# Cross attention with its queries in front of the sums and a group's output products together; self-attention with wide scores and a joined side step

## The chip, the cores and the metric

The kernel runs on one NeuronCore of a Trainium2 chip. The metric is the device time of one execution in microseconds (us), the median of three runs. A core has five engines that each take their instructions in order: TensorE (PE: matrix products; PEld is its loading of the stationary operand), VectorE (DVE), ScalarE (ACT), GpSimd (POOL) and SyncE (SP, which only issues DMAs here). TensorE writes its results to PSUM, eight banks of 2 KiB on each of 128 partitions; VectorE and ScalarE read them from there. GpSimd works on the on-chip memory (SBUF) alone.

## The reference

The program is a decoder of four layers. Each layer has an attention, a cross attention and a feed-forward part, and after each the residual is added and the rows are normalized. The input `x` has 16 batches of 256 tokens with 128 features; the context `ctx_1024` has 64 tokens a batch. Everything is computed in fp32 as far as this change is concerned.

Three cross attentions, in layers 0, 2 and 3, have 16 heads of 8 features and a softmax over the 64 context tokens. In layer 3 the cross attention is followed by a self-attention over the 256 tokens of a batch, also with 16 heads of 8 features:

```python
q = _split_heads(x @ qw + qb)
k = _split_heads(ctx @ kw + kb)
v = _split_heads(ctx @ vw + vb)
scores = jnp.einsum('bqhd,bkhd->bhqk', q, k) / np.sqrt(D // H).astype(np.float32)
...
probs = jax.nn.softmax(scores, axis=-1)
out = jnp.einsum('bhqk,bkhd->bqhd', probs, v)
```

`ca = _mha(input_tensor, ctx_tensor, ...)` gives the cross attention, `sa = _mha(x, x, ...)` the self-attention; each is followed by an output product, residual and normalization.

## The kernel before

The program is written stage by stage on one core. `x` stays on the chip twice: `xt` holds tokens on partitions, `xT` holds features on partitions. Tokens are worked on in 8 groups of 512, a group being two batches. Two stages are concerned.

**`cross_attention` (line 523)** serves the three cross attentions: `layer_x0` (with `side`, which puts the end of layer 0's recurrence, `scan` and `turn`, between the steps), `layer_x2`, and `layer_last` (with a mask and an extra scaling of the scores, lines 582 to 585). Its loop runs over batches `b`, with six steps more at the end. A step does:

- `scores(b + 1)`: for each of four 32-row strips `i` and two halves `u`, a product of 32 rows (heads 4i to 4i+3) with the masked keys `kb` as stationary operand and 256 query columns. `kb`, made by GpSimd in `keys`, holds the keys four times, each time with all but one head of a strip set to zero. The result fills two PSUM tiles `sc` of two banks; ScalarE takes the exponential into `e`.
- `settle`: the last step of a pending normalization (line 404 on ScalarE, 407 on VectorE).
- `sums(b)`: numerators (`vx` as stationary operand) and denominators (a constant) for all heads into one bank `nd`; `normalized` (line 1966) takes the reciprocal `rcT` and multiplies into `oTn`, both on VectorE.
- `keys(b + 2)`; at even `b` `queries(b // 2 + 1)`, a product of 512 columns and its eviction to `qT` on VectorE; at `b % 4 == 1` `values`, four products and their evictions into `vx`.
- `out_product` (line 635) for batch `b - 1`: two products with the output weights into half of bank `y`; after the second batch of a group, `finish` adds the residual (`r`) and starts the normalization, whose reciprocal root (line 383) is on GpSimd.
- `transposed`: four transposes of a finished group and a copy to `xT` on ScalarE.

PSUM is divided by tags. Each call takes four banks for `sc` and one for `y`; with `side` one for `nd` and two for `m`, without `side` two for `nd` and one for `m`. `queries`, `values` and `transposed` share `m`.

**`self_attention` (line 1856)** takes four steps `j` for each batch `n`, each with four heads. A step issues the scores of the next step, then `aside(n, j)`, then its sums. `scores(n, j)` makes eight products, for two halves `t` of the keys and four strips `i`: masked keys `kb[n][r, j, 128 t: ...]` as stationary operand, 256 query columns moving. `sums` makes eight products into `nd`; after the fourth step `nd` is copied (`nds`), the denominators' reciprocal `rcs` is made on VectorE and the numerators are put together in `vas` on GpSimd. `aside` holds everything else, each piece with one bank `m` for all:

- `divided(n - 1)` at `j == 1`: a product with a constant (`swap`) brings the reciprocals to their rows; VectorE multiplies into `oTs`.
- `batch(n + 1)` at `j == 2`: the value product, its evictions into `vs` (four on VectorE), and the masked keys `kb` (one GpSimd instruction, line 1894).
- `project` at even `n`: keys of the next group at `j == 0`, queries at `j == 3`.
- at odd `n`: `out` at `j == 0`, `transposed` at `j == 3`.

Order on TensorE is written out by hand: inside `in_order` every matrix instruction is chained to the one before it (`put`, line 304). The order on the other engines is made by a scheduler when the program is built; the hand-written marks `behind` only add to it. A pool of `bufs` tiles is used in turn, and a new tile waits for all readers of the one before it in the same buffer. `work` tiles have two buffers unless another number is given.

Of the kernel before, what the change touches and what calls it, by code (L numbers as in the profile page):

```python
# [16 lines left out]
ALU = mybir.AluOpType  # L17
# [5 lines left out]
NG = NT // 512  # L23
# [499 lines left out]
def cross_attention(s, wq, wk, wv, wo, bq, bk, bv, finish, mask=None, side=None):  # L523
# [14 lines left out]
    q, kb, es, oT, y = {}, {}, {}, {}, {}  # L538
# [58 lines left out]

    if side is None:
        side = lambda b, late: None
        few, more = 2, 1  # L600
    else:
        few, more = 1, 2
    with s.banks(sc=(2, 2), nd=(few, 1), y=(1, 1), m=(more, 1)), s.in_order(), s.deferring():
# [11 lines left out]
        for b in range(B + 6):  # L615
# [3 lines left out]
            side(b, False)  # L619
            if b < B:  # L620
                sums(b)
            side(b, True)
            if b + 2 < B:
                keys(b + 2)
                if b % 2 == 0:
                    queries(b // 2 + 1)
                if b % 4 == 1 and b + 3 < B:
                    values(b // 4 + 1)
            if 1 <= b <= B:
                out_product(s, y, oT, b - 1, wo, finish)  # L630
            if b % 2 == 1 and b >= 5 and b // 2 - 2 < NG:
                s.transposed(b // 2 - 2)


def out_product(s, y, oT, b, wo, finish):

    if b % 2 == 0:
        y[b // 2] = s.bank("y", [128, 4, D])
    for t in range(2):
        s.mm(y[b // 2][:, 2 * (b % 2) + t, :], oT[b][:, 128 * t:128 * t + 128], wo)  # L640
    if b % 2 == 1:
        finish(b // 2, y[b // 2])
# [1213 lines left out]
def self_attention(s, wq, wk, wv, wo, bq, bk, bv, finish):  # L1856
# [7 lines left out]

    nc = s.nc
# [10 lines left out]
    q, k, kb, es, oT, nd, va, rc = {}, {}, {}, {}, {}, {}, {}, {}  # L1876
# [7 lines left out]
    def batch(n):  # L1884
        ps = s.bank("m", [128, 2, 256])
        for t in range(2):
            s.mm(ps[:, t, 0:128], s.xT[:, S * n + 128 * t:S * n + 128 * t + 128], wv)
        pv = ps[:, :, 0:128].rearrange("p t (i j d) -> p t i j d", i=4, j=4)
# [3 lines left out]
        kb[n] = s.work("kb4", [128, 4, S])  # L1892
        o = S * (n % 2)
        nc.gpsimd.tensor_tensor(kb[n], k[n // 2][:, o:o + S].unsqueeze(1).broadcast_to([128, 4, S]), hm4, ALU.mult)

    def scores(n, j):
        o = S * (n % 2)
        sc = [s.bank("sc", [128, 2, 2, S]) for _ in range(2)]
        for t in range(2):
            for i in range(4):  # L1900
                r = slice(32 * i, 32 * i + 32)
                s.mm(sc[i // 2][:, i % 2, t, :], kb[n][r, j, 128 * t:128 * t + 128], q[n // 2][r, o:o + S])
# [4 lines left out]
    def sums(n, j):  # L1907
        if j == 0:
            nd[n] = s.bank("nd", [128, 2, S])
        for t in range(2):  # L1910
# [27 lines left out]
    def aside(n, j):  # L1938

        g = n // 2  # L1940
        if j == 1 and 1 <= n <= B:
            divided(n - 1)
        if j == 2 and n + 1 < B:
            batch(n + 1)
# [63 lines left out]
```

## Time and profile before

| what | us |
|---|---|
| median of the runs (2226.88, 2229.49, 2230.01) | 2229.49 |
| the profiled execution's own time | 2229.6 |
| its span from the first instruction to the last | 2227.8 |
| TensorE busy in the span | 1795.3 |
| reciprocals `rcT` in the cross attentions, 48 of 1751 ns | 84.1 |
| exponentials `e` of the self-attention, 128 of 1021 ns | 124.0 |
| VectorE `rcs` reciprocals of the self-attention, 16 of 1753 ns | 28.0 |

The page of the profile gives busy time per engine and groups of equal instructions by line, engine, tile and shape. A group's row reads: count, busy time, mean length of one in ns, then the engine's idle time just before them and what ended it. `out<-in` names the tile written and the tiles read. An fp32 product appears as two records, each with its own load of the stationary operand. `32*128 32x256` means a stationary operand of 32 rows by 128 columns and a moving one of 32 rows by 256 columns. Two kinds of query are used besides: the waits (who waited for whom, total, times, longest) and the timeline (start, length, engine, line, tiles, count, and in brackets the engine's idle time before it with its releaser). TensorE's clock is granted in two rates; the share granted is a column of the busy time by stretch. Ends of matrix products are modelled, so lengths overlap, and steps are best read from start to start.

### The profile page before, as it was taken

The page shows a single profiled execution, that of the slowest core. Times are in us where ns is not written, and L with a number is a line of the kernel's source. Part 1 is how long each engine was busy: PE and PEld are TensorE (multiplying, and loading weights), DVE is VectorE, ACT ScalarE, POOL GpSimd, SP SyncE. Part 2 cuts the span into 40 slices and gives each one's busy share as a digit, 9 for nine tenths or more (in the row PEclk, how much of TensorE's full clock was granted, in tenths as well). Part 3 has the DMA queues.
Part 4 walks back from the last instruction along what each step waited for, and adds up shares of the span by engine and source line. Part 5 has one row for each costly group of instructions (what it writes and reads, how often), then busy time and mean ns, then how long its engine had stood idle before and what let it go on. Part 6 is the DMA issues. An engine that isn't in the chain of part 4 may idle for free.

```text
span 2227.8 us, 39433 instructions
## 1 busy us (share of the span) xinstructions
PE 1795.3 (81%) x16572; PEld 1132.3 (51%) x16572; DVE 1133.0 (51%) x2808; ACT 857.9 (39%) x1267; POOL 811.0 (36%) x956
## 2 busy tenths in 40 slices
PE   6784388886999836949784789987789988999998
PEld 3451256664777624625452556654445544555554
DVE  5677624544366663145476677746725552322231
ACT  6565633432333201322354222225646653223221
POOL 2432322222244325755434334444536652111110
PEclk8896569997999956969896899988979998999999
DMA  3000000001011221430000000010000000000000
GB/s 114 4 3 21 1 2 3 3 3 45 1 30 29 71 51 45 76 88 0 6 14 20 1 1 1 2 41 23 2 1 2 2 1 1 5 5 5 5 10 10
DMA packets 45649, 41.59 MB, mean 19 GB/s; under 512 B 6880, under 2 KB 42144, under 8 KB 44832
## 3 DMA queue, kind: packets, MB, share of 16 engines
q1 hardware_dynamic: 35456, 31.22, 4.5%
q0 software_dynamic: 5632, 4.33, 1.5%
q10 hardware_dynamic: 4384, 3.52, 0.5%
q8 instruction: 130, 2.13, 0.4%
q14 instruction: 47, 0.39, 0.1%
HBM read 28.44 MB, written 10.62 MB: 18 GB/s over the span
## 4 chain that ended last, share of the span: by engine, by line
PE 56%; DVE 18%; POOL 11%; issue 7%; ACT 5%; DMA 2%; POOLq 0%; DVEq 0%; SPq 0%; ACTq 0%
PE p L336 14%; PE m L336 12%; PE sc L336 11%; PE y L336 6%; PE nd L336 3%; POOL rs L383 2%; PE nd L340 2%; PE den L340 2%; DVE rcT L1969 2%; PE m L343 2%; POOL acc L1318 2%; PE num L336 2%; DVE st L393 1%; ACT xt L404 1%; DVE r L458 1%
## 5 line engine op out<-in xcount | busy, mean ns | idle before, releaser
L336 PE MATMUL p<-h,w_f 128*128 128x512 f32 x512 | 222.3, 592 | 0.4 <-DVE h L1820 0.4
L336 PE MATMUL sc<-qT,kb 32*128 32x256 f32 (+1 forms) x2816 | 184.3, 381 | 42.6 <-DVE qT L650 17.2
L381 POOL TENSOR_SCALAR ve<-mv 128x4 f32<-128x4 f32 x128 | 30.6, 239 | 427.1 <-DVE mv L394 423.7
L336 PEld LDWEIGHTS sc<-qT,kb 32*128 32x128 f32 x2816 | 129.6, 204 | 94.3 <-issue 61.2
L343 PE MATMUL m<-ident,xt 128*128 128x128 f32 x448 | 87.8, 318 | 104.0 <-ACT xt L404 47.4
L336 PEld LDWEIGHTS p<-h,w_f 128*128 128x128 f32 x512 | 96.7, 190 | 119.8 <-issue 117.9
L1905 ACT ACTIVATE e<-sc 128x1024 f32<-128x1024 f32 x128 | 124.0, 1021 | 74.2 <-PE sc L336 73.4
L383 POOL TENSOR_TENSOR rs<-ve,nhalf 128x4 f32<-128x4 f32 x128 | 134.3, 1049 | 6.3
L343 PEld LDWEIGHTS m<-ident,xt 128*128 128x128 f32 x448 | 59.1, 156 | 132.9 <-ACT xt L404 54.8
L393 DVE BATCH_NORM_STATS2 st<-r 128x6 f32<-128x128 f32 x480 | 119.6, 272 | 3.3
L435 POOL TENSOR_TENSOR xb<-xt,r_x 128x512 f32<-128x512 f32 x48 | 60.8, 1271 | 152.2 <-DVE r L1763 76.9
L1969 DVE RECIPROCAL rcT<-nd 128x256 f32<-128x256 f32 x48 | 84.1, 1751 | 62.3 <-PE nd L336 62.3
L355 ACT COPY xT<-m 128x512 f32<-128x512 f32 x104 | 60.0, 581 | 139.2 <-PE m L343 138.5
L404 ACT ACTIVATE xt<-r,nm,rs 128x128 f32<-128x128 f32 x176 | 72.5, 484 | 95.0 <-POOL nm L399 95.0
L1825 ACT ACTIVATE h<-p,w_f 128x512 f32<-128x512 f32 x64 | 44.0, 687 | 153.6 <-PE p L336 153.5
L336 PE MATMUL m<-xT,w_a 128*128 128x512 f32 x144 | 82.0, 685 | 25.7 <-DVE vxs L910 18.9
L407 DVE TENSOR_SCALAR xt<-r,mv,rs 128x128 f32<-128x128 f32 x208 | 66.8, 382 | 59.6 <-POOL rs L383 59.6
L1831 DVE TENSOR_TENSOR ys<-y,r_f 128x512 f32<-128x512 f32 x8 | 5.5, 691 | 175.4 <-PE y L336 175.4
L578 ACT ACTIVATE e<-sc 128x1024 f32<-128x1024 f32 x64 | 61.9, 1019 | 62.6 <-PE sc L336 62.6
L1626 DVE TENSOR_TENSOR a<-sc,cst 128x1024 f32<-128x1024 f32 x64 | 75.0, 1208 | 14.4 <-PE sc L336 14.3
L394 DVE BATCH_NORM_AGGREGATE mv<-st 128x2 f32<-128x6 f32 x512 | 80.7, 167 | 0.1
L1094 ACT ACTIVATE e<-sc 128x1024 f32<-128x1024 f32 x32 | 32.8, 1024 | 110.0 <-PE sc L336 110.0
(423 smaller groups left out, 4075.2 us busy)
## 6 DMA issues: line engine op xcount, KB each, us to landing
acc<-xt SPq DMA_DIRECT2D x16, 256.0 KB, 2.8
mw<-in_moe SPq DMA_DIRECT2D x8, 512.0 KB, 4.1
yx<-acc SPq DMA_DIRECT2D x12, 256.0 KB, 3.6
w_f<-in_w_f SPq DMA_DIRECT2D x1, 2824.0 KB, 10.5
w_x<-in_w_x SPq DMA_DIRECT2D x1, 2336.5 KB, 9.8
xt<-in_x SPq DMA_DIRECT2D x8, 256.0 KB, 7.5
rows<-xn SPq DMA_DIRECT2D x8, 256.0 KB, 2.5
out_x<-xt SPq DMA_DIRECT2D x8, 256.0 KB, 2.3
```

What stands on the lines that cost most here:

```text
L336: self.put(self.nc.tensor.matmul(out=out, lhsT=lhsT, rhs=rhs, start=start, stop=stop))
L340: self.put(self.nc.tensor.matmul(out=out, lhsT=lhsT, rhs=rhs, start=start, stop=stop, skip_group_check=True))
L343: self.put(self.nc.tensor.transpose(out, in_, self.ident if ident is None else ident))
L383: nc.gpsimd.tensor_tensor(rs, ve, self.nhalf[:, :n], ALU.pow)
L393: nc.vector.bn_stats(st[:, j, :], r[:, j, :])
L394: nc.vector.bn_aggr(mv[:, j, :], st[:, j, :])
L404: ins, front = nc.scalar.activation(out[:, j, :], r[:, j, :], AF.Identity, bias=nm[:, j:j + 1], scale=rs[:, j:j + 1]), self.latest
L407: ins, front = nc.vector.tensor_scalar(out[:, j, :], r[:, j, :], mv[:, j, 0:1], rs[:, j:j + 1], ALU.subtract, ALU.mult), self.mark
L578: s.latest = nc.scalar.activation(eu, sc[h], AF.Exp, scale=8 ** -0.5)
L1626: s.mark = nc.vector.tensor_tensor(a[:, h, :, :], sc[h].rearrange("p i j k -> p (i j) k"), tri, ALU.mult)
L1905: nc.scalar.activation(e[:, 2 * h:2 * h + 2, :, :], sc[h], AF.Exp, scale=8 ** -0.5)
L1969: s.nc.vector.reciprocal(rc, nd[:, 1, :])
```

## The change

In `cross_attention`, `queries(b // 2 + 1)` is issued between the scores of `b + 1` and the sums of `b`, at even `b`. The output products of a group's two batches are no longer made one batch a step but all four at the even step that follows the group's second batch, in a new `out`, ahead of `values` and `transposed`. The bank `y` is gone: `out` takes its bank from `m`, which has three banks with `side` and two without. `oTn` has three buffers.

In `self_attention`, queries are masked instead of keys (`qb`), and scores are made with 128 keys as stationary operand and the masked queries of two heads, 512 columns, as moving one: four products a step instead of eight. A step now covers half of the keys for two heads, where it covered all keys for one head of each strip; `sums` follows that. The value product of the next batch and the `swap` product of the last one are put in the two halves of one bank at `j == 1`, with `divided` and `batch` behind them. Queries are projected at `j == 0` and keys at `j == 2`.

```diff
@@ -535,7 +535,7 @@
         nc.gpsimd.memset(t, 0.0)
     on = s.c["on2"].rearrange("p (u k) -> p u k", u=2)
     hm4 = s.c["hm4"].unsqueeze(2).broadcast_to([128, 4, SC])
-    q, kb, es, oT, y = {}, {}, {}, {}, {}
+    q, kb, es, oT = {}, {}, {}, {}
 
     def values(g):
         ps = s.bank("m")
@@ -595,12 +595,16 @@
                          es[b][:, i, u, :], u == 0, u == 1)
         oT[b] = normalized(s, nd)
 
+    def out(g):
+        y = s.bank("m", [128, 4, D])
+        for j in range(4):
+            s.mm(y[:, j, :], oT[2 * g + j // 2][:, 128 * (j % 2):128 * (j % 2) + 128], wo)
+        finish(g, y)
+
+    few = 1
     if side is None:
-        side = lambda b, late: None
-        few, more = 2, 1
-    else:
-        few, more = 1, 2
-    with s.banks(sc=(2, 2), nd=(few, 1), y=(1, 1), m=(more, 1)), s.in_order(), s.deferring():
+        side, few = lambda b, late: None, 2
+    with s.banks(sc=(2, 2), nd=(few, 1), m=(4 - few, 1)), s.in_order(), s.deferring():
         side(-1, False)
         for g in range(2):
             ps = s.bank("nd")
@@ -617,29 +621,19 @@
                 scores(b + 1)
             s.settle()
             side(b, False)
+            if b % 2 == 0 and b + 2 < B:
+                queries(b // 2 + 1)
             if b < B:
                 sums(b)
             side(b, True)
             if b + 2 < B:
                 keys(b + 2)
-                if b % 2 == 0:
-                    queries(b // 2 + 1)
-                if b % 4 == 1 and b + 3 < B:
-                    values(b // 4 + 1)
-            if 1 <= b <= B:
-                out_product(s, y, oT, b - 1, wo, finish)
+            if b % 2 == 0 and 2 <= b <= B:
+                out(b // 2 - 1)
+            if b % 4 == 1 and b + 3 < B:
+                values(b // 4 + 1)
             if b % 2 == 1 and b >= 5 and b // 2 - 2 < NG:
                 s.transposed(b // 2 - 2)
-
-
-def out_product(s, y, oT, b, wo, finish):
-
-    if b % 2 == 0:
-        y[b // 2] = s.bank("y", [128, 4, D])
-    for t in range(2):
-        s.mm(y[b // 2][:, 2 * (b % 2) + t, :], oT[b][:, 128 * t:128 * t + 128], wo)
-    if b % 2 == 1:
-        finish(b // 2, y[b // 2])
 
 
 def evac_dve(s, out, ps, bias=None):
@@ -1873,7 +1869,7 @@
     hm4 = s.c["hm4"].unsqueeze(2).broadcast_to([128, 4, S])
     lo, hi = s.c["half"][:, 0:1], s.c["half"][:, 1:2]
     row = bv.rearrange("p (i j d) -> p i j d", i=4, j=4)
-    q, k, kb, es, oT, nd, va, rc = {}, {}, {}, {}, {}, {}, {}, {}
+    q, k, qb, es, oT, nd, va, rc = {}, {}, {}, {}, {}, {}, {}, {}
 
     def project(d, n, g, wt, bias):
         ps = s.bank("m")
@@ -1881,25 +1877,28 @@
         d[g] = s.work(n, [128, 512])
         evac_dve(s, d[g], ps, bias)
 
-    def batch(n):
-        ps = s.bank("m", [128, 2, 256])
+    def product(n, ps):
+        ps = ps.rearrange("p (t c) -> p t c", t=2)
         for t in range(2):
-            s.mm(ps[:, t, 0:128], s.xT[:, S * n + 128 * t:S * n + 128 * t + 128], wv)
-        pv = ps[:, :, 0:128].rearrange("p t (i j d) -> p t i j d", i=4, j=4)
+            s.mm(ps[:, t, :], s.xT[:, S * n + 128 * t:S * n + 128 * t + 128], wv)
+
+    def batch(n, ps):
+        ps = ps.rearrange("p (t c) -> p t c", t=2)
+        pv = ps.rearrange("p t (i j d) -> p t i j d", i=4, j=4)
         for j in range(4):
             nc.vector.tensor_tensor(vxs[n % 3][:, :, :, 40 * j:40 * j + 8], pv[:, :, :, j, :],
                                     row[:, :, j, :].unsqueeze(1).broadcast_to([128, 2, 4, 8]), ALU.add)
-        kb[n] = s.work("kb4", [128, 4, S])
+        qb[n] = s.work("kb4", [128, 4, S])
         o = S * (n % 2)
-        nc.gpsimd.tensor_tensor(kb[n], k[n // 2][:, o:o + S].unsqueeze(1).broadcast_to([128, 4, S]), hm4, ALU.mult)
+        nc.gpsimd.tensor_tensor(qb[n], q[n // 2][:, o:o + S].unsqueeze(1).broadcast_to([128, 4, S]), hm4, ALU.mult)
 
     def scores(n, j):
-        o = S * (n % 2)
+        o = S * (n % 2) + 128 * (j % 2)
         sc = [s.bank("sc", [128, 2, 2, S]) for _ in range(2)]
-        for t in range(2):
-            for i in range(4):
-                r = slice(32 * i, 32 * i + 32)
-                s.mm(sc[i // 2][:, i % 2, t, :], kb[n][r, j, 128 * t:128 * t + 128], q[n // 2][r, o:o + S])
+        for i in range(4):
+            r = slice(32 * i, 32 * i + 32)
+            s.mm(sc[i // 2][:, i % 2, :, :].rearrange("p h k -> p (h k)"), k[n // 2][r, o:o + 128],
+                 qb[n][r, j - j % 2:j - j % 2 + 2, :].rearrange("p h k -> p (h k)"))
         e = es[n, j] = s.work("e", [128, 4, 2, S])
         for h in range(2):
             nc.scalar.activation(e[:, 2 * h:2 * h + 2, :, :], sc[h], AF.Exp, scale=8 ** -0.5)
@@ -1907,10 +1906,12 @@
     def sums(n, j):
         if j == 0:
             nd[n] = s.bank("nd", [128, 2, S])
-        for t in range(2):
+        t = j % 2
+        for u in range(2):
             for i in range(4):
-                s.part(nd[n][32 * i:32 * i + 32, j // 2, :], vxs[n % 3][:, t, i, 32 * j:32 * j + 32],
-                       es[n, j][:, i, t, :], j == t == 0, j % 2 == 1 and t == 1)
+                h = j - t + u
+                s.part(nd[n][32 * i:32 * i + 32, j // 2, :], vxs[n % 3][:, t, i, 32 * h:32 * h + 32],
+                       es[n, j][:, i, u, :], j == u == 0, t == u == 1)
         if j == 3:
             sb = s.work("nds", [128, 2, S])
             nc.vector.tensor_copy(sb, nd[n])
@@ -1923,11 +1924,9 @@
                 nc.gpsimd.tensor_scalar(sb[:, u, :], sb[:, u, :], m, None, ALU.mult)
             nc.gpsimd.tensor_tensor(va[n], sb[:, 0, :], sb[:, 1, :], ALU.add)
 
-    def divided(n):
-        ps = s.bank("m", [128, 2, S])
-        s.mm(ps[:, 0, :], s.c["swap"], rc[n])
+    def divided(n, ps):
         oT[n] = s.work("oTs", [128, S], bufs=4)
-        nc.vector.tensor_tensor(oT[n], va[n], ps[:, 0, :], ALU.mult)
+        nc.vector.tensor_tensor(oT[n], va[n], ps, ALU.mult)
 
     def out(g):
         y = s.bank("m", [128, 4, D])
@@ -1938,12 +1937,17 @@
     def aside(n, j):
 
         g = n // 2
-        if j == 1 and 1 <= n <= B:
-            divided(n - 1)
-        if j == 2 and n + 1 < B:
-            batch(n + 1)
-        if n % 2 == 0 and j in (0, 3) and g + 1 < NG:
-            project(*((q, "qT", g + 1, wq, bq) if j else (k, "kTs", g + 1, wk, bk)))
+        if j == 1 and n <= B:
+            ps = s.bank("m", [128, 2, S])
+            if n + 1 < B:
+                product(n + 1, ps[:, 1, :])
+            if n >= 1:
+                s.mm(ps[:, 0, :], s.c["swap"], rc[n - 1])
+                divided(n - 1, ps[:, 0, :])
+            if n + 1 < B:
+                batch(n + 1, ps[:, 1, :])
+        if n % 2 == 0 and j in (0, 2) and g + 1 < NG:
+            project(*((q, "qT", g + 1, wq, bq) if j == 0 else (k, "kTs", g + 1, wk, bk)))
         if n % 2 == 1 and j == 0 and 1 <= g <= NG:
             out(g - 1)
         if n % 2 == 1 and j == 3 and 2 <= g <= NG + 1:
@@ -1952,7 +1956,9 @@
     with s.banks(sc=(3, 2), nd=(1, 1), m=(1, 1)), s.in_order():
         project(q, "qT", 0, wq, bq)
         project(k, "kTs", 0, wk, bk)
-        batch(0)
+        ps = s.bank("m", [128, 2, S])[:, 1, :]
+        product(0, ps)
+        batch(0, ps)
         scores(0, 0)
         for n in range(B + 4):
             for j in range(4):
@@ -1967,7 +1973,7 @@
 
     rc = s.work("rcT", [128, S], bufs=1)
     s.nc.vector.reciprocal(rc, nd[:, 1, :])
-    oT = s.work("oTn", [128, S])
+    oT = s.work("oTn", [128, S], bufs=3)
     s.nc.vector.tensor_tensor(oT, nd[:, 0, :], rc, ALU.mult)
     return oT
 
```

## The prediction

> **What bounds the kernel now.** I read the page's head first, then each engine's busy time in the four stretches that the diff touches, then TensorE's waits in each, then the order of its work inside one period.
>
> ```profile
> span 2227.8 us, 39433 instructions
> ...
> PE 1795.3 (81%) x16572; PEld 1132.3 (51%) x16572; DVE 1133.0 (51%) x2808; ACT 857.9 (39%) x1267; POOL 811.0 (36%) x956
> ```
> ```profile
> 67.00:176.00 109.00, 83.67 (x946) 52.29 (x946) 74.55 (x200) 59.73 (x100) 39.33 (x72) 0.91 0.03 8
> 1085.00:1182.00 97.00, 78.06 (x900) 46.11 (x898) 62.10 (x153) 46.25 (x69) 29.65 (x52) 0.93 0.06 20
> 1512.00:1624.00 112.00, 83.08 (x904) 48.06 (x904) 76.11 (x156) 69.58 (x89) 52.43 (x74) 0.88 0.00 1
> 1624.00:1826.00 202.00, 190.77 (x2255) 104.50 (x2255) 95.81 (x246) 127.13 (x135) 106.45 (x95) 0.96 0.01 2
> ```
> Columns of the second: stretch, its length, busy TensorE, weight loads, VectorE, ScalarE, GpSimd, granted clock, DMA. The rows are the cross attentions of layers 0, 2 and 3 (x0, x2, x3 below), then the self-attention. No DMA matters in them. Self-attention is TensorE-bound, 191 of 202 us. The cross attentions leave TensorE 19 to 29 us idle each, with VectorE 62 to 76 us busy. Who ends those waits in x2:
>
> ```profile
> PE sc L336 <- DVE qT L650: 8.9, 8, 1.3
> PE m L343 <- DVE vx L554: 3.9, 2, 1.9
> ```
> Scores wait each pair of batches for the queries' eviction (`qT`); a transpose waits twice for the one `m` bank that `values` still holds. x0 and x3 show 8.4 and 8.3 us of the first, x3 4.0 of the second. In self-attention the timeline of TensorE (start, length) shows one wait per two batches:
>
> ```profile
> 1698.88 1.15 PE L336 MATMUL sc<-qT,kb 32*128 32x256 f32 x16
> 1699.95 0.70 PE L336 MATMUL m<-rcs,cst 128*128 128x256 f32 x2
> 1700.58 1.07 PE L340 MATMUL nd<-e,vs 128*32 128x256 f32 x16
> 1701.58 1.15 PE L336 MATMUL sc<-qT,kb 32*128 32x256 f32 x16
> 1704.04 0.71 PE L336 MATMUL m<-w_x,xT 128*128 128x128 f32 x4 [1.31 <-DVE oTs L1930]
> 1704.68 1.07 PE L340 MATMUL nd<-e,vs 128*32 128x256 f32 x16
> ```
> From start to start: scores 1.08, sums 1.00, swap 0.63, value product 0.64. The product waits 1.31 us because the swap result in the same bank is read by `oTs`, which stands on VectorE behind the normalization (`r`, L407), which waits for GpSimd.
>
> **Self-attention, part by part.** *Wide scores.* Sixteen records of 256 columns become eight of 512, half the weight loads; streamed columns are the same. Four row groups start within 21 ns of each other, the next four 216 ns later; records of 512 columns in plain products follow each other every 429 ns (32 records `p<-h` take 13.90 us, the last 0.59 alone). So a phase changes from 4 x 216 to 2 x 429: 6 ns, times 64 = -0.4. [...] The trace shows each load begun while the row group before it streams, so I take 0.4. [...] The 256-column rows overlap fully; no row here has 32 rows by 512. [...]
> *Joined aside.* Value product and swap follow each other without the load-and-drain edge between a tiled and a full phase: a product before another full phase takes 0.54, before sums 0.64; 15 x 0.10 = -1.5. The product now stands before the swap, so it no longer waits for `oTs`: six waits (1.42 and five of 1.31) go, -8.0. Where does that stall go? `oTs` ends 4.03 us after the swap's start (1703.98 against 1699.95). The next user of `m` in an odd batch is now the transpose, about 1.17 + 2 x 2.08 = 5.3 us after the joined aside begins; `vs` adds 0.61, and the bank is free at about 5.1 at the latest. In an even batch it is the key projection after 3.25, with `oTs` and `vs` done by 2.3. No wait returns there.
> *Emptied steps.* Fourteen steps now have no aside. Such steps exist already (1683.80: scores 1.30 long in place of 1.08) because the third score buffer waits for an exponential: 14 x 0.22 = +3.1.
> *Masked queries.* GpSimd multiplies queries instead of keys, same shape, 1.89 us, in the same place of its queue; queries are projected first. At the start the multiply no longer waits for the keys (1630.04), so first scores come at about 1631.4 instead of 1632.07: -0.7.
> Sum: -0.4 - 1.5 - 8.0 + 3.1 - 0.7 = **-7.5**.
>
> **Cross attention.** On TensorE alone, x2's pair of 9.56 us (1130.28 to 1139.84) is 8.52 of work and 1.04 of wait for `qT`. After: scores 1.08, queries 1.07 (0.11 more between tiled phases), sums 1.86, eight output products together 1.09, scores 1.08, sums 1.86, transpose 0.59 = 8.63. The merging itself is worth nothing: before, each half lay beside another full phase (0.61 + 0.55). But another loop runs at nearly the old pace:
>
> ```profile
> 1127.80 1.76 DVE L1969 RECIPROCAL rcT<-nd 128x256 f32<-128x256 f32 x1 [2.65 <-PE nd L336]
> 1129.48 0.65 DVE L650 TENSOR_SCALAR qT<-m,w_x 128x512 f32<-128x512 f32 x1
> 1130.05 0.41 DVE L1971 TENSOR_TENSOR oTn<-nd,rcT 128x256 f32<-128x256 f32 x1
> 1130.38 0.68 DVE L458 TENSOR_TENSOR r<-y,xb 128x512 f32<-128x512 f32 x1
> ...
> 1136.04 0.69 DVE L1507 TENSOR_REDUCE sx<-xt 128x4 f32<-128x512 f32 x1 [0.93 <-ACT xt L404]
> 1136.64 0.41 DVE L1971 TENSOR_TENSOR oTn<-nd,rcT 128x256 f32<-128x256 f32 x1
> ...
> 1137.37 1.76 DVE L1969 RECIPROCAL rcT<-nd 128x256 f32<-128x256 f32 x1 [0.24 <-PE nd L336]
> ```
> The chain is `r`, statistics, GpSimd (2.05 us), ScalarE `xt` (1.65), then `sx`, which VectorE takes in order ahead of `oTn`, `qT`, `rcT` and the next `r`. It repeats every 9.56 us with 0.24 idle. The new program's VectorE order moves `qT` ahead of `rcT` and `r` ahead of `oTn`, but `sx` stays: **9.32**, not 8.63. So an ordinary pair saves 0.24. The moved `qT` itself is covered: sums and output products, 2.95 us, lie between queries and the scores that read it, of which eviction and latency take 0.8 once VectorE is free; without that cover the old 1.04 is back.
> *x2.* The first `qT` wait, 1.3, goes entire; the early pair without `sx` saves 0.4; four ordinary pairs save 1.0. The two pairs with `values` (12.78, 12.59) lose the 1.94 wait for `vx`. The second bank gives `values` and the transpose one each, and the next queries wait for `vx` instead, about 0.9, with sums, output products and all later work of TensorE queued behind; such a pair falls to 10.6: -4.2. The last output is eight products instead of four and the sums before it start later: +0.9. Sum -6.0; I take **-5.5**, since coupled queues only add waits.
> *x3.* The loop is sums, `rcT` (starts 2.05 after sums, 1.76), `qT`, `oTn`, `r`, statistics, `e` (L582), two exponentials, next even sums: 9.94 us. Without `qT` it is 9.37. But here the last statistic moves behind the 1.27 us `e`, so GpSimd and ScalarE come later; over sums, normalization, transposed copy, L584, L585, an odd batch's sums come 14.85 us after those of the even batch three before; 4.60 of TensorE later come the next even ones: two pairs in 19.4, 9.7 each. Two ordinary pairs save 0.25 each; the two with `values` fall from 13.45 and 13.0 to 10.9: -4.6; the first `qT` wait -1.2; tail +0.4. Sum -5.9, taken as **-5.5.**
> *x0.* One `nd` bank here, so the odd batch's `oTn` holds the next sums. From `rcT` of an even batch over `r`, statistics, the recurrence's `r`, its statistics, the odd `rcT`, `oTn`, sums and back, a pair takes 10.6; `qT` leaves it: -0.55. Three ordinary pairs with recurrence work -1.6, the two with `values` also lose transposes' waits for `xT` (1.49, 0.77): -3.4 with their 0.55; start -1.4. Pairs without recurrence gain nothing: `r` ahead of `oTn` delays the odd sums, +0.2. Tail +0.5. Prologue: GpSimd now finishes all gate products before the first normalization, whose statistics end at about 56.4 instead of 51.5; followed through `xt`, `kT`, `kb` to the `xT` copies, scores start about 1.5 later: +1.5, between -2 and +4. Sum -4.2; I take **-3.5**.
>
> Together -7.5 - 5.5 - 5.5 - 3.5 = -22.0 on the span of 2227.8: 2205.8. This execution took 2229.6, 1.8 outside the span, and stands at the median 2229.5. **2207.6 us.** The clock's half-rate windows (0.88 to 0.96 granted above) may fall elsewhere; one that covers a 3.4 us stretch of full TensorE work costs about 1.7, both ways, and is left to the range.
>
> **Rivals.** *TensorE's sums alone set the pace:* no loop binds. Then x2 gains 10.7, x3 13, x0 14, self-attention 10.6: 2181. For it: VectorE still waits 12.0 us for sums in x2's second half. Against: the loop above has 0.24 us to give. *The loops keep all of the cross attentions,* queries in front only moving the wait: self-attention's -7.5 stays, 2222. For it: VectorE is 76 of 112 us busy in x3, with more in order behind each wait. *Slower: wide scores don't run four at a time.* Place: the 64 score phases, on the path since TensorE is 94% busy. [...]
>
> **Chances.** Forecast case (2198 to 2217) 0.62; TensorE alone or near it (2180 to 2198) 0.13; loops keep all (2217 to 2225) 0.15; wide scores partly serial 0.10, of which half within 0.2% or below, half slower. A run of this kernel tells 0.2% (4.5 us) from no change. Faster 0.90, same 0.05, slower 0.05. Range 2192 to 2221, leaving about 1 in 10 on each side.
>
> **What would show it.** Right: no `batch` product waiting for `oTs`; score phases of about 1.07 us; some 14 scores waiting for `e`; x2 pairs near 9.3 and TensorE waiting there for `qT` or an exponential instead; self-attention near 194 us. Wrong: score phases over 1.15; x2 pairs at 8.7 (loop misjudged) or 9.6; `r` waiting for `out`; a changed clock in these stretches.

## The result, and the profile after

The changed kernel takes 2197.24 us (median of four runs, 2193.24 to 2200.10) against 2228.84 (2226.88 to 2230.01): 31.6 us less, ratio 0.9858, 95% interval 0.9839 to 0.9877. A second, later comparison gave 2199.90 against 2232.12, ratio 0.9851 (0.9811 to 0.9890). The forecast was 2207.6, -21.9: right in direction, 10 us too small. The sum hides larger errors of both signs, and those are what the experiments are about.

The head of the page after the change:

```profile
span 2193.6 us, 38398 instructions
...
PE 1782.1 (81%) x16059; PEld 1102.1 (50%) x16060; DVE 1131.9 (52%) x2808; ACT 855.2 (39%) x1267; POOL 810.2 (37%) x956
```

TensorE has 513 records fewer; 512 of them are scores of the self-attention. Next, busy time by stretch, once for each kernel, over the four stages that the diff touches. The stretches are set by landmarks in TensorE's order: layer 0's, layer 2's and layer 3's cross attention (x0, x2, x3) begin with the first product of the context, the self-attention with its first projection. The columns are as before: stretch, length, busy TensorE, weight loads, VectorE, ScalarE, GpSimd, granted clock, DMA. The kernel before:

```profile
53.57:176.75 123.18, 91.78 (x969) 56.83 (x969) 84.33 (x229) 66.42 (x116) 49.96 (x88) 0.87 0.04 13
1078.51:1193.56 115.05, 84.66 (x918) 49.49 (x917) 66.58 (x169) 52.98 (x81) 37.23 (x62) 0.87 0.05 17
1502.00:1624.26 122.26, 87.60 (x918) 50.32 (x917) 79.25 (x162) 71.74 (x92) 62.37 (x92) 0.86 0.04 17
1624.26:1825.93 201.67, 190.69 (x2255) 104.42 (x2255) 95.81 (x246) 126.92 (x134) 106.38 (x95) 0.96 0.01 2
```

The changed one:

```profile
57.58:179.68 122.10, 93.36 (x969) 56.04 (x969) 83.36 (x233) 65.70 (x114) 48.13 (x86) 0.88 0.02 7
1076.42:1183.00 106.58, 84.85 (x918) 48.48 (x917) 66.22 (x169) 52.52 (x81) 37.11 (x62) 0.87 0.05 18
1491.21:1603.24 112.03, 84.40 (x918) 48.55 (x917) 78.97 (x162) 70.62 (x92) 62.34 (x92) 0.90 0.05 19
1603.24:1792.27 189.03, 186.51 (x1743) 78.27 (x1743) 95.26 (x246) 126.90 (x134) 106.06 (x95) 0.97 0.00 1
```

Read the first number of each row: x0 -1.1, x2 -8.5, x3 -10.2, self-attention -12.6. Before x0 the row starts 4.0 later. In x2 busy TensorE hardly moves (84.66 to 84.85): what went was waiting. In x3 it is 3.2 us less (87.60 to 84.40) for the same 918 records, at a granted clock of 0.90 instead of 0.86, so up to 3.2 of the 10.2 us are the clock; in x0 it is 1.6 more. The stages that were not touched took 5.0 us less between x0 and x2 in this execution: two stretches, which begin near 390 and 867 us, are 3.0 and 2.9 us shorter, with a clock of 0.95 instead of 0.93 and of 0.84 instead of 0.81. In the second trace of the same program the same stages took 2.1 us more; more on that below.

TensorE's waits in x2 (who waited, line, for whom; total, times, longest):

```profile
...
PE m L336 <- ACT xT L355: 3.6, 2, 2.0
PE m L343 <- ACT xt L404: 3.3, 2, 2.0
PE m L336 <- DVE oTn L1977: 2.3, 2, 1.6
PE sc L336 <- DVE qT L644: 1.4, 1, 1.4
...
```

The eight waits of scores for `qT` (8.9 us) have become one, and the two transposes that waited for `vx` (3.9) are gone. In their place two queries wait 2.0 and 1.6 us for `xT`, ScalarE's copy of the transposes. The timeline of TensorE shows where, in a pair of batches with `values` and in the ordinary pair behind it:

```profile
1135.43 1.16 PE L336 MATMUL m<-w_x,ctx 128*128 128x128 f32 x8
1136.43 0.60 PE L343 MATMUL m<-ident,xt 128*128 128x128 f32 x4
1136.96 1.15 PE L336 MATMUL sc<-qT,kb 32*128 32x256 f32 x16
1139.72 1.12 PE L336 MATMUL m<-xT,w_x 128*128 128x512 f32 x2 [1.61 <-ACT xT L355]
1140.77 1.07 PE L336 MATMUL nd<-e,vx 128*32 128x256 f32 x16
...
1147.25 1.15 PE L336 MATMUL sc<-qT,kb 32*128 32x256 f32 x16
1148.33 1.13 PE L336 MATMUL m<-xT,w_x 128*128 128x512 f32 x2
1149.38 1.07 PE L336 MATMUL nd<-e,vx 128*32 128x256 f32 x16
```

From the even sums at 1140.77 to the next at 1149.38 the ordinary pair takes 8.61 us with no wait in it: TensorE's own sum was 8.63. The forecast had said 9.32.

In the self-attention one step of the joined aside looks like this:

```profile
1693.29 1.16 PE L336 MATMUL m<-w_x,oTs 128*128 128x128 f32 x8
1694.38 1.07 PE L340 MATMUL nd<-e,vs 128*32 128x256 f32 x16
1695.38 1.14 PE L336 MATMUL sc<-kb,kTs 32*128 32x512 f32 x8
1696.45 0.38 PE L336 MATMUL m<-w_x,xT 128*128 128x128 f32 x1
```

The wide scores begin at 1695.38, the value product behind them at 1696.45: 1.07 us a phase, and no wait for `oTs`.

### The profile page after: what moved, and what is told of

The parts are those of the page before. It is cut to its first block, busy times and chain, and to the rows that moved or that the text cites. A ratio compares the mean times of both kernels' runs of the same rounds, so it can differ in the third digit from the quotient of the medians.

```text
span 2193.6 us, 38398 instructions
## 1 busy us (share of the span) xinstructions
PE 1782.1 (81%) x16059; PEld 1102.1 (50%) x16060; DVE 1131.9 (52%) x2808; ACT 855.2 (39%) x1267; POOL 810.2 (37%) x956
## 4 chain that ended last, share of the span: by engine, by line
PE 59%; DVE 17%; POOL 9%; issue 7%; ACT 4%; DMA 1%; POOLq 0%; DVEq 0%; ACTq 0%; SPq 0%
PE p L336 14%; PE m L336 13%; PE sc L336 12%; PE y L336 6%; PE nd L336 3%; PE nd L340 3%; POOL rs L383 2%; PE den L340 2%; DVE st L393 2%; PE m L343 2%; POOL acc L1312 2%; PE num L336 2%; DVE r L458 1%; ACT xt L404 1%; DVE e L963 1%
## 5 line engine op out<-in xcount | busy, mean ns | idle before, releaser
L336 PEld LDWEIGHTS p<-h,w_f 128*128 128x128 f32 x512 | 96.9, 190 | 119.9 <-issue 118.0
L1904 ACT ACTIVATE e<-sc 128x1024 f32<-128x1024 f32 x128 | 124.0, 1021 | 61.7 <-PE sc L336 59.5
L336 PE MATMUL sc<-qT,kb 32*128 32x64 f32 (+1 forms) x1792 | 103.8, 356 | 26.9 <-POOL kb L888 7.9
L336 PEld LDWEIGHTS sc<-qT,kb 32*128 32x128 f32 x1792 | 77.7, 208 | 48.7 <-issue 16.7
L578 ACT ACTIVATE e<-sc 128x1024 f32<-128x1024 f32 x64 | 61.9, 1019 | 49.7 <-PE sc L336 49.7
L336 PE MATMUL sc<-kb,kTs 32*128 32x512 f32 x512 | 79.0, 652 | 0.0
```

The lines of the kernel that those rows point to most:

```text
L336: self.put(self.nc.tensor.matmul(out=out, lhsT=lhsT, rhs=rhs, start=start, stop=stop))
L578: s.latest = nc.scalar.activation(eu, sc[h], AF.Exp, scale=8 ** -0.5)
L1904: nc.scalar.activation(e[:, 2 * h:2 * h + 2, :, :], sc[h], AF.Exp, scale=8 ** -0.5)
```

## Experiments

Stage times below are read from each kernel's trace between the landmarks named above; "start" is all that lies ahead of x0, "A" what lies between x0 and x2, "B" between x2 and x3. A and B are the same program in every kernel. Times in us; the ratio is to runs of the kernel before on the same chip, with its 95% interval.

| kernel | start | x0 | A | x2 | B | x3 | self | ratio |
|---|---|---|---|---|---|---|---|---|
| before | 53.6 | 123.2 | 901.8 | 115.1 | 308.4 | 122.3 | 201.7 | 1 |
| changed | 57.6 | 122.1 | 896.7 | 106.6 | 308.2 | 112.0 | 189.0 | 0.9858 (0.9839 to 0.9877) |
| changed, again | 57.5 | 122.1 | 903.9 | 106.3 | 308.2 | 112.0 | 189.0 | 0.9851 (0.9811 to 0.9890) |
| cross attention alone | 57.0 | 121.8 | 903.5 | 106.5 | 308.2 | 112.0 | 201.6 | 0.9931 (0.9903 to 0.9958) |
| self-attention alone | 53.2 | 123.2 | 899.9 | 116.6 | 308.4 | 125.4 | 192.4 | 0.9967 (0.9951 to 0.9983) |
| queries in front alone | 52.8 | 129.2 | 900.5 | 119.7 | 308.6 | 129.2 | 201.6 | 1.0075 (1.0038 to 1.0112) |
| outputs merged, own bank | 52.8 | 129.9 | 903.4 | 115.4 | 313.2 | 123.6 | 200.8 | 1.0055 (1.0037 to 1.0073) |
| outputs merged, shared banks | 56.9 | 124.5 | 890.7 | 105.3 | 313.0 | 112.3 | 201.2 | 0.9934 (0.9913 to 0.9955) |
| transposes at even steps | 57.3 | 119.9 | 915.6 | 101.3 | 314.0 | 106.5 | 186.2 | 0.9862 (0.9827 to 0.9897) |
| the same, again | 57.3 | 119.5 | 918.9 | 101.8 | 313.6 | 106.5 | 186.2 | 0.9860 (0.9833 to 0.9887) |
| queries in front in every second pair | 57.0 | 121.5 | 903.5 | 102.1 | 312.8 | 108.6 | 192.1 | 0.9860 (0.9826 to 0.9893) |
| `sx` twice | 57.8 | 122.2 | 903.9 | 109.3 | 312.5 | 111.8 | 188.9 | one run, 2209.49 us |
| wide scores alone | 53.8 | 123.2 | 903.5 | 116.6 | 308.3 | 125.4 | 201.2 | 1.0000 (0.9982 to 1.0018) |
| joined aside alone | 53.9 | 123.2 | 904.3 | 116.6 | 312.0 | 125.2 | 192.9 | 0.9960 (0.9945 to 0.9975) |

The first row deserves a caution. In three other kernels x2 and x3 are the old program too (self-attention, wide and joined alone), and there they took 116.6 and 125.2 to 125.4, against 115.1 and 122.3 in the trace of before. Measured against those the new cross attentions gain 10 and 13 us, not 8.5 and 10.2. The difference is mostly the clock: in the kernel with wide scores TensorE was busy 1.3 us longer in x2 and 3.1 in x3 than before, with the same records, at 0.85 and 0.84 instead of 0.87 and 0.86.

### The two halves of the change

*Cross attention alone* is the changed kernel with the old `self_attention`.

> The new cross attentions with the old self-attention. Theory A (the forecast: the loop through the normalization holds an ordinary pair of batches in layer 2 at 9.3 us): -14.5 us against the kernel before, about 2214. Theory B (read from the changed kernel's trace: TensorE's own sum, 8.6 us, sets those pairs, and layer 0 loses what its start costs): layer 0 about +3, layer 2 about -8.5, layer 3 about -10, so -16 us from these stages; with what the clock does in stages that were not touched (between -5 and +5), 2207 to 2219. Layer 2's ordinary pairs in the trace decide: 9.3 for A, 8.6 for B.

2214.61 against 2231.35, -16.7. Layer 2's ordinary pairs are 8.30 and 8.61 us (a third, 10.26, has a half-rate stretch of 3.4 us in it): theory B, although A's total was nearer.

*Self-attention alone* is the kernel before with the new `self_attention`.

> The new self-attention with the old cross attentions. The forecast's sum is -7.5 us, about 2221. The changed kernel's trace shows -12.6 in this stage, of which some 2.9 us are one half-rate stretch of the clock that lay at the start of the stage before: if that is chance, -9 to -10 us (about 2219); if the stage truly gains all of it, -12.6 (about 2216). The period of two batches: 24.32 us before, 23.4 by the forecast's terms, 22.97 if the joined aside saves on both products.

2223.36 against 2231.35, -8.0. The stage takes 192.4, -9.3. A half-rate stretch of the clock covers the first 17.9 us of the stage here and 17.8 in the kernel before (1615 to 1642 there); in the changed kernel it ends 10.8 us into the stage (1594 to 1614), and with transposes at even steps, below, after 2.1. The times of the same new stage follow in order: 192.4, 189.0, 186.2, that is 0.47 and then 0.33 us for each microsecond of half rate. So the program gains 9.3, and 3.3 of the 12.6 is the clock. Why the stretch ends earlier was not tried.

### Which part of the cross attention carries the gain

*Queries in front alone*, on the kernel before:

```diff
+            if b % 2 == 0 and b + 2 < B:
+                queries(b // 2 + 1)
             if b < B:
                 sums(b)
...
-                if b % 2 == 0:
-                    queries(b // 2 + 1)
```

> The kernel before with nothing changed but the place of the queries: between the scores and the sums, one or two banks as before, output products two at a time. If the place of the queries alone carries the gain of the cross attentions: -14 to -18 us. If the second bank is what it needs (with one bank the queries now wait for the copy of the transposes, which were issued only one score phase, 1.08 us, before): the wait of 1.04 us for qT turns into one of 1 to 2 us for xT in each pair, and the time is between -4 and +8 us of the kernel before.

2245.24 against 2231.35: 13.9 us slower, outside what either reading allowed. TensorE's waits over x2 in this kernel, and the stage's row of busy times:

```profile
PE m L336 <- ACT xT L355: 5.6, 2, 2.8
PE m L343 <- DVE vx L554: 4.3, 2, 2.3
...
PE m L336 <- DVE vx L554: 2.5, 2, 1.5
PE sc L336 <- DVE qT L650: 1.2, 2, 0.9
```
```profile
1082.45:1202.15 119.70, 88.67 (x917) 50.29 (x917) 66.10 (x169) 52.87 (x81) 37.19 (x62) 0.84 0.05 16
```

The waits for `qT` have shrunk from 8.9 us to 1.2, but 12.4 us of waits for the one bank `m` stand in the other three rows, where 5.4 stood before (transposes 3.9, the first queries 1.5). Two queries wait 2.8 us each for the copy `xT`, and everything behind them on TensorE waits with them. With the waits for `oTn` (1.8 us before, 3.4 now) that is 17.0 us where 16.1 stood: the wait moved, and nothing was gained. Most of what the stage lost is TensorE's own time: it was busy 4.0 us longer for the same work (88.67 against 84.66) at a clock of 0.84 instead of 0.87, and 3.5 and 4.9 us longer in x0 and x3. Why the clock was lower was not shown.

*Outputs merged, with shared banks,* and queries behind the sums as before:

```diff
-            if b % 2 == 0 and b + 2 < B:
-                queries(b // 2 + 1)
             if b < B:
                 sums(b)
...
                 keys(b + 2)
+                if b % 2 == 0:
+                    queries(b // 2 + 1)
```

(on the new cross attention; the self-attention is the old one)

> The new cross attentions with the queries back behind the sums; outputs together and shared banks stay; self-attention as before. If the place of the queries carries the gain: the 8 waits for qT of about 1 us stay in each layer, and only the two waits for vx (3.9 us in layer 2, 4.0 in layer 3) go: -4 to -8 us. If banks and merged outputs carry it: -14 to -18 us. If they cost something by themselves: within 2 us of the kernel before.

2215.03 against 2231.35, -16.3: the same as with queries in front. TensorE's timeline in x2, a pair with `values`:

```profile
1131.34 1.16 PE L336 MATMUL m<-w_x,ctx 128*128 128x128 f32 x8
1132.34 0.60 PE L343 MATMUL m<-ident,xt 128*128 128x128 f32 x4
1132.87 1.15 PE L336 MATMUL sc<-qT,kb 32*128 32x256 f32 x16
...
1138.41 1.15 PE L336 MATMUL sc<-qT,kb 32*128 32x256 f32 x16 [0.59 <-DVE qT L644]
```

Transposes follow `values` without a wait, and the wait for `qT` is still there, between 0.6 and 1.6 us. Pairs with `values` take 10.3 and 10.6 us from even sums to even sums, ordinary ones 9.0 to 9.35; with queries in front 11.4 to 11.9, and 8.3 to 8.7. The queries' place takes half a microsecond off one kind and puts one on the other: nothing in x2 (105.3 and 106.5) and x3 (112.3 and 112.0), 2.7 us in x0.

*Outputs merged, in a bank of their own,* is the last kernel with this line changed back in kind:

```diff
-        y = s.bank("m", [128, 4, D])
+        y = s.bank("y", [128, 4, D])
...
-    with s.banks(sc=(2, 2), nd=(few, 1), m=(4 - few, 1)), ...
+    with s.banks(sc=(2, 2), nd=(few, 1), y=(1, 1), m=(3 - few, 1)), ...
```

> The kernel with queries behind the sums and a group's output products together, now in a bank of their own (one), with two banks for the rest in layer 0 and one in layers 2 and 3, as in the kernel before: the merging alone. If merging alone is worth nothing, as the forecast put it: layers 2 and 3 at 114 to 117 and 121 to 124 us, like the kernel before. If the merging gives the gain (1.09 us of output products stand between the queries and the scores that read them, where 0.61 stood): waits for qT fall from 1.04 to about 0.6 to 0.9, some 2 to 3 us a layer, 112 and 119. If banks give nothing: 105 and 112, like the kernel with shared banks.

2246.19 against 2234.85, 11.3 us slower: x2 115.4 and x3 123.6 as in the kernel before, x0 6.7 longer, and the untouched B 4.8 longer at a clock of 0.84 instead of 0.87. Its waits over x2, then the row of x2 in this kernel and in the one with shared banks:

```profile
PE sc L336 <- DVE qT L644: 7.4, 8, 1.5
PE m L343 <- DVE vx L554: 4.8, 2, 2.4
```
```profile
1086.05:1201.49 115.44, 85.86 (x917) 50.30 (x917) 66.58 (x169) 52.98 (x81) 37.25 (x62) 0.85 0.05 17
1072.11:1177.38 105.27, 81.45 (x918) 48.32 (x917) 66.59 (x169) 52.52 (x81) 37.18 (x62) 0.89 0.05 18
```

So with queries behind, x2 is 10.2 us shorter with the shared bank (115.4 to 105.3), x3 11.2 and x0 5.4. In x2 the waits for `vx` are gone (4.8 us of transposes and 1.5 of a query); 4.4 of the 10.2 us, and 5.4 of the 11.2 in x3, are TensorE's busy time at a higher clock, and that sharing causes the higher clock was not shown. Sharing is the one edit of the three that gains. It was tried only with merged outputs; from reading the program, output products spread over two steps would hold a bank across them.

### The new wait, and what stands behind it

*Transposes at even steps,* on the changed kernel:

```diff
+            if b % 2 == 0 and b >= 6 and b // 2 - 3 < NG:
+                s.transposed(b // 2 - 3)
             if b % 4 == 1 and b + 3 < B:
                 values(b // 4 + 1)
-            if b % 2 == 1 and b >= 5 and b // 2 - 2 < NG:
-                s.transposed(b // 2 - 2)
```

> The changed kernel with the transposes of a group moved from the odd step, where they stand just ahead of the next queries, to the even step behind the output products. If queries wait only because they get the bank that the transposes have just filled: the waits of queries for xT (3.6 us in layer 2, 4.1 in layer 3, 8.2 in layer 0) go, and the kernel gains 5 to 9 us on the changed kernel. If the loop through the normalization stands right behind that wait: 0 to 2 us.

In x2 and x3 the waits for `xT` inside the pairs went: pairs with `values` fall from 11.4 and 11.9 us to 9.8 and 9.3 in x2 and from 12.1 to 9.7 in x3; the stages lose 5.0 and 5.5 us. In x0 the waits for `xT` grew, from 8.2 to 11.0 us, while those of sums for `oTn` fell from 7.5 to 3.9; that stage lost 2.2. But the whole took 2203.87 beside 2199.90 for the changed kernel: no gain that these runs can tell. A and B, which are the same program in both, took 17.6 us more. The repeat:

> The kernel with transposes at the even step once more, in more rounds. Its three cross attentions and the self-attention took 16 us less than the changed kernel's beside it, and its layer 1 and the part behind layer 2, which are the same program, 18 us more, in half-rate stretches of the clock. If that was chance of one execution: -35 to -45 us against the kernel before (ratio near 0.982). If what the stages gain is given back to the clock each time: the ratio stays at 0.985 to 0.987.

2205.33 against 2234.85, ratio 0.9860: given back again, with A at 918.9. Most of it is in one stretch of layer 1's attention. Its row in three kernels, first with transposes at even steps (the repeat), then the changed kernel (the second trace), then outputs merged with shared banks:

```profile
311.30:554.10 242.80, 197.35 (x4212) 141.76 (x4208) 113.04 (x222) 84.45 (x123) 58.64 (x68) 0.87 0.03 11
```
```profile
313.10:544.70 231.60, 186.15 (x4212) 134.72 (x4208) 113.08 (x222) 84.44 (x123) 58.88 (x68) 0.91 0.04 12
```
```profile
315.30:537.00 221.70, 176.59 (x4212) 129.46 (x4208) 113.03 (x222) 84.44 (x123) 58.84 (x68) 0.95 0.04 12
```

Same 4212 records, same work on the other engines, and 242.8, 231.6 and 221.7 us as the granted clock is 0.87, 0.91 and 0.95. What the pairs gained is there in both traces, and it was paid back by the clock in layer 1 and behind x2 (0.84 instead of 0.87 there). That the faster stages cause it was not shown: why this program meets the lower clock there in both traces stays open.

*Queries in front in every second pair,* layers 2 and 3 only:

```diff
+            late = few == 2 and b % 4 == 2
-            if b % 2 == 0 and b + 2 < B:
+            if b % 2 == 0 and b + 2 < B and not late:
                 queries(b // 2 + 1)
...
                 keys(b + 2)
+                if late:
+                    queries(b // 2 + 1)
```

> The changed kernel, layers 2 and 3 alone altered: queries in front of the sums in every second pair, and behind the sums in the pairs that follow values and transposes. From the traces of the changed kernel (ordinary pair 8.6 us, pair with values 11.4) and of the one with queries behind (9.1 and 10.3): 8.6 and 10.3, so -1 us per pair with values, -2 us in each of the two layers, -4 in all. If a loop of two pairs holds the sum of both: 0 to -1.

The pairs came about as read from the two parents, 8.5 and 10.0 to 10.3 in x2, 9.1 to 9.4 and 10.1 to 10.8 in x3, and the stages gained 4.2 and 3.5 us, twice what was expected. The kernel took 2201.82, no better than the changed one: B was 4.7 longer and the self-attention met the longer half-rate stretch at its start (192.1).

### Is the loop through the normalization near?

*`sx` twice:* the reduction `nc.vector.tensor_reduce(sx, xg, ...)` in layer 2's preparation of integers stands there two times.

> The changed kernel with the row maximum sx of layer 2, 0.69 us on VectorE, made twice; the second is work that leaves the result as it is. Theory A (the loop through the normalization, with sx in it, holds the pairs): each ordinary pair of layer 2 grows from 8.6 to 9.2 or 9.3 us and the stage by 3.5 to 4.5 us. Theory B (TensorE's sum holds the pairs and the loop has slack): ordinary pairs stay at 8.6 to 8.7, the stage grows by under 1 us.

Between the two. The ordinary pair stayed at 8.61, as B has it, but the stage grew by about 3 us (106.3 and 106.6 to 109.3), which is nearer to A. One pair with `values` went from 11.36 to 12.08; the other, together with the ordinary pair behind it, from 22.1 to 22.8 (a half-rate stretch lies in the two): about the length of one `sx` each, and the end of the stage grew as well. TensorE's waits for `qT` went from 1.4 to 3.1, for `oTn` from 2.3 to 3.3, for `xT` from 3.6 to 4.0. So the loop does not hold the ordinary pairs, but elsewhere in the stage a longer one costs. In the changed kernel VectorE runs like this around an ordinary pair (brackets: its idle time before):

```profile
1142.78 1.76 DVE L1975 RECIPROCAL rcT<-nd 128x256 f32<-128x256 f32 x1 [1.14 <-PE nd L336]
1144.45 0.63 DVE L458 TENSOR_TENSOR r<-m,xb 128x512 f32<-128x512 f32 x1
...
1150.16 0.69 DVE L1501 TENSOR_REDUCE sx<-xt 128x4 f32<-128x512 f32 x1 [1.60 <-ACT xt L404]
```

The next even `rcT` starts at 1151.83, 9.05 us after 1142.78, while TensorE's pair takes 8.61. The chain does fall behind by 0.44 a pair; it starts 1.14 early here, because the pair with `values` before it was longer, and two ordinary pairs would use up only 0.88. With `sx` twice, as an estimate, a chain of 9.05 + 0.69 us falls 1.13 behind in one pair, which the 1.14 just covers: the pair at 8.61 there fits that.

### The self-attention's parts

*Wide scores alone:* masked queries, which are projected ahead of the keys, four products of 512 columns, sums to fit; each side step keeps its own bank.

> The kernel before with wide scores alone (masked queries, four products of 512 columns a step, sums to fit); the side steps stay where they were, one bank each. If four row groups of 512 columns stream at once: a score phase of 1.07 us as before (1.08), the six waits for oTs stay, the self-attention stays within 1.5 us of its 201.7. [...]

2235.79 against 2234.85, ratio 1.0000 (0.9982 to 1.0018). The timeline of TensorE:

```profile
1707.70 1.14 PE L336 MATMUL sc<-kb,kTs 32*128 32x512 f32 x8
1710.18 0.71 PE L336 MATMUL m<-w_x,xT 128*128 128x128 f32 x4 [1.34 <-DVE oTs L1932]
```

A phase is 1.07 us (1705.00 to 1706.07), the wait for `oTs` is still 1.34.

*Joined aside alone:* value product and swap in one bank at the second step, masked keys and narrow scores as before.

> The kernel before with the joined aside alone: value product and swap in one bank at the second step, queries projected at the third; masked keys and narrow scores stay. The six waits for oTs go (-8.0), value product and swap together take 1.08 us instead of 1.27 (15 times, -2.9), 13 more emptied steps cost 0.22 each (+2.9): the self-attention at 193 to 194 us, the kernel at -8. If the wide scores are what lets the joined aside pay: above 197.

2225.73 against 2234.85, -9.1; the stage 192.9, at the edge of the 193 to 194 expected, and 0.5 us from that of the whole new self-attention. The pair of products:

```profile
1720.35 0.71 PE L336 MATMUL m<-w_x,xT 128*128 128x128 f32 x4
1720.90 0.60 PE L336 MATMUL m<-rcs,cst 128*128 128x256 f32 x2
1721.43 1.07 PE L340 MATMUL nd<-e,vs 128*32 128x256 f32 x16
```

0.55 and 0.53 from start to start, where they took 0.64 and 0.63 apart. The joined aside alone makes 8.7 of the self-attention's 9.3 us.

*The changed kernel again,* beside its variants:

> The changed kernel, unaltered, beside the variants of this group: -31 us against the kernel before if the first comparison holds. The parts run so far gave -16.7 (cross attention alone) and -8.0 (self-attention alone): if they add and nothing else happens, -25.

2199.90 against 2232.12, -32.2: the two halves run alone add to only -24.7. Of the 7.5 between, 3.3 is the clock at the start of the self-attention; the rest is not placed, and the intervals of the two halves (6.1 and 3.6 us to each side) would hold it.

## Why the prediction was right, and where it was wrong

**Self-attention, -7.5; the program gains 9.3.** *Wide scores -0.4:* right, 1.07 us a phase. Halving the weight loads of the scores (1024 records and 49.6 us busy in the kernel before, 512 and 24.7 in the changed one) was worth nothing: with wide scores alone the ratio is 1.0000. Four 32-row products of 512 columns ran all four at once: in the changed kernel's trace the four of the step at 1695.38 start within 20 ns of each other, the next four 532 ns after the first, and the phase takes 1.07 us. *Six waits for `oTs`, -8.0:* right; one wait came in, 0.54 us for `qT` at the first `product` (1661.75). *Emptied steps +3.1:* about right; 16 score phases of 1.30 us stand there, 4 before: +2.6. *Joined aside -1.5:* mis-sized. The step counted one edge between a tiled and a full phase, 0.10 us; joining saves 0.19 (1.27 to 1.08), 15 times 0.19 is -2.9. *Start -0.7:* -0.8. These make -8.9; the last 0.4 us was not followed.

**x2 and x3, -5.5 each; -8.5 and -10.2 measured, 3.2 of the latter in TensorE's busy time at a higher clock.** *The loop holds an ordinary pair at 9.32* is the step that failed. Its links are as described, and in the changed kernel the chain takes 9.05; but a slower chain sets the pace only once its slack is gone. Here every second pair in the middle of the stage is about three microseconds longer on TensorE and gives the chain its lead back. The text gave 8.7 as the sign of this error, and 8.61 was seen. *A pair with `values` falls to 10.6 because queries wait 0.9 for `vx`* failed the other way: 11.4 to 11.9 in x2, 12.1 in x3, with waits of 1.5 to 2.0 for `xT`. The description of the kernel said that a pool's tiles are used in turn; the built program gives these queries the bank of the transposes just ahead of them, not the bank of `values`. In the trace they wait on ScalarE's semaphore alone, which the transposes' copy sets, while in an ordinary pair queries behind transposes wait on VectorE's. Moving the transposes took the wait away. *The merging itself is worth nothing* holds for x2 and x3 and was 6.7 us too kind for x0. *What the queries' place is worth* (the first wait 1.3, 0.24 a pair) was booked to the wrong edit: by itself the kernel came out 13.9 us slower, and on top of shared banks it is worth 0.4 in the whole kernel, which is within the noise.

**x0, -3.5 with its prologue; +2.9 measured.** The prologue was put at +1.5 between -2 and +4; it is +4.0, at the edge. VectorE's first `r` runs at 52.80 instead of 45.57, and ScalarE's first `xt` at 58.72 instead of 54.30. All kernels with shared banks have it (56.9 to 57.8), all others not (52.8 to 53.9); why the order of the prologue depends on them was not tried. In the stage, the sum left out that queries would wait for `xT`. TensorE's waits there:

```profile
PE m L336 <- ACT xT L355: 8.2, 6, 2.5
PE nd L336 <- DVE oTn L1977: 7.5, 7, 2.6
```

Waits for `qT` fell by 7.5 us (8.4 to 0.9) and the one for `kT` by 3.0 (4.4 to 1.4). Against that, waits for `xT` grew by 4.0 (4.2 to 8.2, queries and transposes together), those for `oTn` by 2.6 (sums and output products) and TensorE's busy time by 1.6; -5.0 for the stage became -1.1.

So the terms add up as: self-attention 5.1 more than forecast (3.3 of it clock), x2 3.0 and x3 4.7 more (3.2 of it clock), x0 with the prologue 6.4 less; the untouched stages add another 5.8 in this trace. The total came within 10 us because x0's error cancels part of the others. That much of it is luck: without those 6.4 us the result would lie near 2191, below the stated range. *Rivals:* TensorE's sums alone setting the pace is what ordinary pairs in x2 do; the pairs with `values` kept the total from its 2181. The loops keeping all of the cross attentions (2222) and the partly serial wide scores are both excluded, the first by -16.7 for the cross attention alone, the second by the ratio 1.0000. That wide scores run partly one after another, a chance of 0.10 in the forecast, was the author's assumption; no run shows it, and a phase took 1.07 us where it had taken 1.08.

## What to carry to other kernels

A chain that is longer than the pace of the bounding engine binds only after its slack is used up (here 9.05 us against 8.61, with 1.14 in hand): work out how much lead the longer iterations give back before taking its period as the iteration time. Where several uses share buffers, look up in the built program which use follows which in one buffer; the wait that a moved step meets is that of its real predecessor. And test an edit of three parts one part at a time: here one part (queries in front) only moves the wait and came out slower by itself, one (merged outputs) gains nothing by itself, and the third (the shared bank) gains.

## What the runs showed of the hardware that was not expected

Half-rate stretches of TensorE's clock (granted 0.50 instead of 1.00) last multiples of 3.41 us in the traces of the kernel before and of the changed one (3.41, 6.83, 10.24, up to 99; only the last one of an execution, 7.53 and 8.09 us, is cut short by its end), and in one execution all begin on one grid of that period: 3.4133 us fits the starts in both traces, and divided by it they leave a remainder of 0.23 to 0.25 us in the kernel before and of 2.99 to 3.01 in the changed one, over the whole 2200 us. Not every such stretch has a long idle gap of TensorE ahead of it: in the changed kernel the one at 1306.88 follows 13.7 us in which the longest gap is 1.07. With transposes at even steps, layer 1 has 6.83 us of it about every 31 us (at 347, 378, 408, 439, 470 and 501), while TensorE has no idle gap over 1.4 us between 311 and 526. Ahead of each of the six lie two windows of the grid in which TensorE was busy 60 to 65% of the time; but with outputs merged and shared banks two such windows (from 397.57 to 404.40, 61 and 60%) were followed by full rate, so what decides it stays open.

In the fourteen traces this one stretch of layer 1 took between 221.7 and 242.8 us. A change upstream moves a later stage on that grid (x2 begins 3.08 us behind a point of the grid in the kernel before, 1.64 in the changed one); whether this is what makes the difference was not tried. A trace's stages that nobody touched have to be read before a difference of 10 us in the total is put down to the edit.
